# Order of the products' parts and of their reads in a fused graph-convolution and attention kernel on one core

## The chip, the core and the metric

The kernel runs on one core of a Trainium2 chip. The metric is the device time of one launch in microseconds. The kernel before took 2282.02 us (median of three runs, 2273.76 to 2284.43).

A core has a matrix engine (TensorE, PE in the profile; its weight loads are PEld), a vector engine (VectorE, DVE), an activation engine (ScalarE, ACT), a general engine (GpSimd, POOL) and a queue engine (SyncE, SP), from which this kernel issues all of its transfers. Each engine runs its own list of instructions in order, and they wait for each other by semaphores.

## The reference

Two layers on x of 128 graphs x 128 nodes x 512 features in fp32, each added to its own input:

```python
h = relu(layernorm(x))
norm_adj = adj * deg_inv_sqrt[:, None] * deg_inv_sqrt[None, :]
x = x + norm_adj @ (h @ weight) + bias

h = relu(layernorm(x))
q, k, v = (h @ W + b for W, b in ((Wq, bq), (Wk, bk), (Wv, bv)))     # 8 heads of 64
scores = q @ k.T / 8 + (1 - adj) * -1e9
x = x + softmax(scores) @ v @ Wo + bo
```

`adj` is one 128 x 128 matrix for all graphs. The five products with 512 x 512 weights are most of the work.

## The kernel before

Four graphs make a group; there are NG = 32 groups. The matrix products with weights multiply a 512 x 512 operand (four graphs, or their transpose) by a 512 x 512 weight.

Each such product is computed by Strassen-Winograd with seven half-size products P1, P5, P2, P6, P3, P7, P4 (`PRODUCTS`, line 31). Three of them (P1, P6, P7) are plain products of four 128 x 256 block matmuls, each in two halves of 64 output rows. The other four are themselves split: P5 and P3 by seven 128 x 128 block matmuls (`SEVEN`, line 80), P2 and P4 by another seven, cut into "phases" of four, two and one (`PHASES`, line 70). Sums of weights and of operands for this are made beforehand, mainly by GpSimd (`combine_one`, L91).

The results go to six PSUM banks: a0 and a1 by turns for the plain products, d0 and d1 for the seven (four blocks in d0, three in d1), b for P2 and c for P4. VectorE, and for first reads ScalarE, adds what the banks hold into the result in SBUF (`add` L437, `read` L447, `first` L726 and L740). Banks accumulate: P3 is added on top of P5 in d0 and d1, and a later phase on top of an earlier, and so a bank is read twice or three times, each time into the next place where Winograd's scheme needs the running sum. A matmul that goes on in a bank therefore has to wait until the reads of its state so far are over. In d0, four blocks lie side by side, and their reads are two columns of blocks (512 wide), single blocks (128 wide) and a diagonal of two blocks (256 wide).

`Projection.step(n)` issues product n's matmuls and its first reads, `rest(n)` the reads that come after whatever the plan has put between. Of P4, phases 1 and 2 are not issued in their own projection: they are kept in `tail` and issued at the start of steps 1 and 2 of the next projection, before that step's own matmuls; their reads follow in the same step. In the projection K the result of P4 is taken differently (`whole`: ScalarE reads part of bank c and adds the bias) and nothing trails.

The main loop goes over t = 0 to 32. In each t come five blocks of seven steps: W (graph convolution of group t + 1), Q, K and V (projections of group t) and Y (output projection of group t - 1). A written plan (`at(t, place, f)`) puts all other work at places such as "Q1" (before step 1 of Q), "Q1b" (between step 1 and its rest). The order of every engine is the order in which the program writes its instructions. The pieces that matter here:

- W3: on SP, the store of the second half of group t - 2 (`store_half` L853), whose last values are the trailing phases of Y read in W1 and W2. The load of the first half of x for group t + 2 (`load_x` L167) comes right after it on SP's queue, and that of the second half at W5.
- Q0b, Q1b, Q3b: the layer statistics of those loads (`ln1`: BATCH_NORM_STATS2 L322, aggregation L323, and L327), on VectorE. The trailing phases of W are issued and read in Q1 and Q2.
- K0b and K3b: statistics of group t + 1 after its convolution (`ln2`), for its first and second half. The normalised rows of the second half are made at V5 and V6.
- V0: attention times v of the group before (L835), then the scores of this group (L769), which VectorE masks and moves from PSUM (L776).
- Y6b or Y3b: the row maximum of the scores' last graph (`row_max` L788) on VectorE, just ahead of W.

Of the kernel before, what the change touches and what calls it, by code (L numbers as in the profile page):

```python
# [68 lines left out]

PHASES = (((0, 0, 0), (3, 6, 1), (2, 2, 2), (1, 1, 3)), ((6, 3, 3), (5, 5, 0)), ((4, 4, 0),))  # L70

# [23 lines left out]
def kernel(  # L95
# [288 lines left out]
    class Projection:  # L384
# [25 lines left out]

        def seven(self, product, fresh):
            i, k = product
            for x, y, b, place in SEVEN:
                self.matmul(
                    bank[f"d{b}"][:, place * P : (place + 1) * P],
                    self.left.slot(i, x),
                    self.right.slot(k, y),
                    fresh and place == 0,
                )

        def phase(self, out, product, n):
            i, k = product
            for m, (x, y, place) in enumerate(PHASES[n]):
                self.matmul(
                    out[:, place * P : (place + 1) * P],
                    self.left.slot(i, x),
                    self.right.slot(k, y),
                    n == 0 and m == 0,
                )
# [9 lines left out]
        @staticmethod  # L439
        def diagonal(dst):  # L440
            d0, d1 = dst[:, 0, 0, :], dst[:, 1, 1, :]
            return bass.AP(d0.tensor, d0.offset, [d0.ap[0], [d1.offset - d0.offset, 2], d0.ap[-1]])

        def read(self, half, y, src):
# [9 lines left out]

        def read_seven(self, half, y, part, first=False):
            dst = self.cut(half, y)
            diagonal = self.diagonal(dst)
            m = [bank[f"d{b}"].rearrange("p (s f) -> p s f", f=P) for b in range(2)]
            columns = m[0][:, 0:2].unsqueeze(2).to_broadcast([P, 2, 2, P])
            if part == 1:  # L460
                self.add(dst[:, 1, 0], m[0][:, 3])
                self.add(diagonal, m[1][:, 1:3])
                self.add(dst[:, 0, 1], m[0][:, 2])
                self.add(diagonal, m[0][:, 2:4], ALU.subtract)
                return
            if first and self.first is not None:
                self.first(dst.rearrange("p j r f -> p r j f"), columns, y)
            else:
                self.add(dst.rearrange("p j r f -> p r j f"), columns)
            self.add(diagonal, m[1][:, 0:1].to_broadcast([P, 2, P]))  # L470

        def read_phase(self, half, y, src, n):
            dst, m = self.cut(half, y), src.rearrange("p (s f) -> p s f", f=P)
            if n == 0:
                self.add(dst[:, :, 0], m[:, 0:2])
                self.add(self.diagonal(dst), m[:, 2:4])
            elif n == 1:
                self.add(dst[:, 0, 1], m[:, 3])
                self.add(dst[:, 0, 1], m[:, 0])
            else:  # L480
                self.add(dst[:, 1], m[:, 0:1].to_broadcast([P, 2, P]))

        def step(self, n):
# [3 lines left out]
            left = tail.pop(0) if n in (1, 2) and tail else None  # L487
            if left:

                left[0]()  # L490
            if n == 0:
# [3 lines left out]
            elif n == 1:  # L495
                if inner:
                    self.seven(P5, True)
                else:
                    self.product(bank["d0"], P5, True)
            elif n == 2:  # L500
                if inner:
                    self.phase(bank["b"], P2, 0)
                else:
                    self.product(bank["b"], P2, True)
            elif n == 3:
                self.product(a, P6, False)
                self.read_first(0, 1, a)
            elif n == 4:
                if inner:
                    self.phase(bank["b"], P2, 1)  # L510
                    if self.whole:
                        self.phase(m, P4, 0)
                    self.seven(P3, False)
                    self.read_phase(0, 0, bank["b"], 1)
                    if self.whole:

                        self.whole(t[:, 0, :], m[:, : 2 * P], 0)
                        self.whole(t[:, 1, P:], m[:, 3 * P :], 1)
                        self.add(t[:, 0, :P], m[:, 2 * P : 3 * P])
                else:  # L520
                    self.product(bank["d0"], P3, False)
            elif n == 5 and self.whole:
                self.phase(m, P4, 1)
                self.product(a, P7, False)
                self.whole(t[:, 1, :P], m[:, 3 * P :], 1)
                self.add(t[:, 1, :P], m[:, :P])
                self.add(t[:, 0, :], a[:, : 2 * P])
# [29 lines left out]
            else:  # L557
                self.product(bank["c"], P4, True)
                self.read(1, 0, bank["c"])
            if left:  # L560
                left[1]()
            if n == 2:
                if inner:
                    self.read_phase(0, 0, bank["b"], 0)
                else:
                    self.read(0, 0, bank["b"])

        def rest(self, n):

            inner = self.inner  # L570
            if n == 1:
                if inner:
                    self.read_seven(1, 1, 0, True)
                else:
                    self.read_first(1, 1, bank["d0"])
            elif n == 2 and inner:
                self.read_seven(1, 1, 1)
            elif n == 4:
                if inner:
                    self.read_seven(0, 1, 0)  # L580
                    self.read_seven(0, 1, 1)
                else:
# [280 lines left out]
    for t in range(-1, NG + 1):  # L863
# [47 lines left out]
        elif 1 <= t + 1 < NG and t >= 0:  # L911
            g = t + 1
            at(t, "K0b" if g < NG - 1 else "Q0b", ln2, g, 0)
            at(t, "K3b" if g < NG - 1 else "Q3b", ln2, g, 1)
            if g == NG - 1:
# [277 lines left out]
```

## Time and profile before

| what | us |
|---|---|
| median of three runs | 2282.02 |
| the profiled execution, whole | 2282.34 |
| its span, first to last instruction | 2280.6 |
| TensorE busy | 2249.9 |
| VectorE busy | 1865.0 |
| GpSimd busy | 1864.7 |
| ScalarE busy | 1391.1 |
| one 128 x 512 read of PSUM by VectorE | 0.68 |
| one 128 x 256 read | 0.42 |
| one 128 x 128 read | 0.28 |

Busy time is summed over the span. A matmul's end is modelled in this profile, so two matmuls that overlap in the pipeline leave no gap between them even where the second began late; the starts of the records are more exact. The granted TensorE clock was 0.998. The transfers moved 565.17 MB, and the 16 DMA engines were busy 83.3% of the time with the kernel's own queue.

### The profile page before, as it was taken

How to read it: one execution, taken by the hardware profiler on the slowest of the kernel's cores; microseconds unless marked ns; L12 is line 12 of the kernel's file. 1: busy time of each engine (PE TensorE's matmuls, PEld its weight loads, DVE VectorE, ACT ScalarE, POOL GpSimd, SP SyncE). 2: the span in 40 equal slices, each digit the busy share in tenths (PEclk: the TensorE clock that was granted, in tenths of full speed). 3: DMA queues.
4: the chain of work that ended last, by engine and by line, in shares of the span. 5: the costliest groups of instructions: out<-in, count | busy, mean ns of one | idle time of the engine just before them, and what ended most of it. 6: DMA issues, size and time to landing. Idle time of an engine off the chain costs nothing.

```text
span 2280.6 us, 79643 instructions
## 1 busy us (share of the span) xinstructions
PE 2249.9 (99%) x32679; PEld 1944.6 (85%) x32679; DVE 1865.0 (82%) x4832; ACT 1391.1 (61%) x3556; POOL 1864.7 (82%) x1928
## 2 busy tenths in 40 slices
PE   9899999999999999999999999999999999999999
PEld 7688888888888888888888888888888888888887
DVE  7778878888888788888888888888888888888876
ACT  4565666656656556666566665565755666655754
POOL 6899888878898788888888887889888888888764
PEclk9999999999999999999999999999999999999999
DMA  5388978889898898889898888988899988899882
GB/s 171 151 259 246 282 243 252 243 251 295 240 267 239 237 290 246 263 243 258 251 275 266 249 244 253 289 252 249 245 254 263 274 265 257 243 255 283 245 239 83
DMA packets 448700, 565.17 MB, mean 248 GB/s; under 512 B 326352, under 2 KB 333648, under 8 KB 447824
## 3 DMA queue, kind: packets, MB, share of 16 engines
q1 hardware_dynamic: 448336, 560.08, 83.3%
q8 instruction: 257, 4.21, 0.7%
q14 instruction: 107, 0.88, 0.1%
HBM read 358.68 MB, written 122.68 MB: 211 GB/s over the span
## 4 chain that ended last, share of the span: by engine, by line
PE 80%; DVE 8%; DMA 8%; issue 1%; POOL 1%; SPq 1%; ACT 0%; DVEq 0%; POOLq 0%
PE bank_a L137 29%; PE bank_d L137 17%; PE bank_b L137 9%; PE bank_c L137 8%; DMA xt<-in_x_dram 7%; PE pa L137 5%; DVE xt L437 3%; PE bank_d L769 3%; PE po L835 2%; DVE xt L447 2%; PE pt L686 1%; PE pss L769 1%; PE bank_b L835 1%; PE bank_a L835 1%; DVE nmx L788 1%
## 5 line engine op out<-in xcount | busy, mean ns | idle before, releaser
L796 ACT ACTIVATE att<-att,nmx 128x128 f32<-128x128 f32 x1024 | 396.5, 391 | 0.8 <-DVE nmx L788 0.8
L137 PE MATMUL bank_a<-op_h,w 128*64 128x256 f32 x2976 | 356.6, 380 | 0.0
L804 POOL TENSOR_TENSOR att<-att,rsm 128x1024 f32<-128x1024 f32 x128 | 242.9, 1898 | 61.0 <-DVE rsm L803 59.3
L137 PEld LDWEIGHTS bank_a<-op_h,w 128*64 128x64 f32 x2976 | 225.7, 137 | 67.0 <-issue 1.2
L437 DVE TENSOR_TENSOR xt<-xt,bank_d 128x512 f32<-128x512 f32 x732 | 268.9, 415 | 14.1 <-PE bank_d L137 0.5
L809 ACT COPY att<-att 128x2048 uint16<-128x2048 uint16 x121 | 229.3, 1895 | 54.4 <-POOL att L804 54.4
L341 ACT ACTIVATE h<-xt,nb,rs 128x512 f32<-128x512 f32 x254 | 207.4, 818 | 74.6 <-POOL nb L330 72.9
L328 POOL TENSOR_TENSOR rs<-ve,mhalf 128x2 f32<-128x2 f32 (+1 forms) x129 | 91.7, 711 | 181.9 <-DVE ve L327 181.2
L726 ACT ACTIVATE q<-bank_a,bqk 128x256 f32<-128x256 f32 x192 | 80.4, 470 | 247.2 <-PE bank_a L137 244.5
L91 POOL TENSOR_TENSOR op_o<-op_o 128x256 f32<-128x256 f32 x297 | 210.4, 733 | 10.0
L137 PE MATMUL bank_d<-op_h,w 128*64 128x128 f32 (+1 forms) x3424 | 215.4, 276 | 2.6 <-issue 0.4
L91 POOL TENSOR_TENSOR op_a<-op_a 128x256 f32<-128x256 f32 x279 | 197.1, 730 | 14.9 <-DVE op_a L373 5.2
L137 PEld LDWEIGHTS bank_d<-op_h,w 128*64 128x64 f32 x3424 | 193.6, 137 | 10.8 <-issue 7.1
L91 POOL TENSOR_TENSOR op_h<-op_h 128x256 f32<-128x256 f32 x270 | 191.0, 731 | 12.4 <-DVE op_h L373 3.1
L322 DVE BATCH_NORM_STATS2 st<-xt 128x6 f32<-128x512 f32 x256 | 173.2, 677 | 31.1 <-DMA xt<-in_x_dram 31.0
L796 ACT ACTIVATION_READ_ACCUMULATOR att<-att,nmx 128x1 f32 x1024 | 194.6, 190 | 0.0
L137 PE MATMUL bank_a<-w,op_o 128*64 128x256 f32 x1536 | 183.9, 379 | 0.0
L137 PE MATMUL bank_a<-w,op_h 128*64 128x256 f32 x1488 | 178.8, 381 | 0.0
L137 PE MATMUL bank_a<-w,op_a 128*64 128x256 f32 x1488 | 176.4, 379 | 0.0
L447 DVE TENSOR_TENSOR xt<-bank_a,xt 128x512 f32<-128x512 f32 x252 | 167.1, 684 | 9.6 <-PE bank_a L137 3.0
L776 DVE SCALAR_TENSOR_TENSOR att<-bank_d,msk 128x512 f32<-128x512 f32 x128 | 82.5, 686 | 102.2 <-PE bank_d L769 94.9
L788 DVE TENSOR_REDUCE nmx<-att 128x8 f32<-128x1024 f32 x128 | 154.9, 1210 | 0.0
(183 smaller groups left out, 5810.1 us busy)
## 6 DMA issues: line engine op xcount, KB each, us to landing
w<-wd_v SPq DMA_DIRECT2D x93, 704.0 KB, 5.9
w<-wd_o SPq DMA_DIRECT2D x93, 704.0 KB, 7.5
w<-wd_q SPq DMA_DIRECT2D x90, 704.0 KB, 6.5
planes<-att SPq DMA_DIRECT2D x121, 512.0 KB, 4.8
w<-wd SPq DMA_DIRECT2D x87, 704.0 KB, 5.8
xt<-in_x_dram SPq DMA_DIRECT2D x63, 512.0 KB, 6.2
out_dram<-xt SPq DMA_DIRECT2D x62, 512.0 KB, 4.4
planes_h<-att SPq DMA_DIRECT2D x29, 512.0 KB, 3.0
```

The source lines that it names most:

```text
L91: engine.tensor_tensor(twice(out), twice(x), twice(y), ALU.subtract if minus else ALU.add)
L137: nc.tensor.matmul(out[y : y + P // 2], lhsT[:, y : y + P // 2], rhs, **flags)
L322: nc.vector.bn_stats(self.st[:, j, :], self.src[:, j, :])
L328: nc.gpsimd.tensor_tensor(self.rs[:, c], self.ve[:, c], mhalf[:, c], ALU.pow)
L341: nc.scalar.activation(h, src[:, j, :], AF.Relu, bias=nb[:, j : j + 1], scale=rs[:, j : j + 1])
L437: nc.vector.tensor_tensor(dst, dst, src, f)
L447: nc.vector.tensor_tensor(t, src.rearrange("p (r f) -> p r f", r=2), t, ALU.add)
L788: nc.vector.tensor_reduce(nmx, att_of(g, b), AX.X, ALU.max, negate=True)
L796: nc.scalar.activation(att[:, h, :], att[:, h, :], AF.Exp, bias=nmx[:, h : h + 1], scale=1.0, accum_out=sm[:, h : h + 1])
L804: nc.gpsimd.tensor_tensor(att, att, rsm.unsqueeze(2).to_broadcast([P, H, P]), ALU.mult)
L809: nc.scalar.copy(planes, halves)
L835: nc.tensor.matmul(po[p * HD : (p + 1) * HD, c * P : (c + 1) * P], vs[g][:, b, h * HD : (h + 1) * HD], aT[:, p * NC + c, :], start=True, s ...
```

## The change

There are four parts.

- In `SEVEN`'s use: the blocks of one product are issued bank by bank. P5 (step 1) issues d0's four, then d1's three; P3 (step 4) d1's three first, then d0's four. Reads of d0 and d1 are split into `read_columns`, `read_three` (d1), `read_across` and `read_minus` and put in an order that begins with d1 (except for the columns in step 1). d1's first read moves from the rest of step 1 to the rest of step 2.
- The trailing phases: phase 1 is issued between d0's and d1's blocks in step 1, phase 2 behind P2's phase 0 in step 2, and the read of phase 2 behind that of bank b.
- `PHASES` gets new places in the bank, with an order of its own for projections whose weights stay (Q and K), so that the reads of the phases are four 256-wide instructions instead of five (three 256-wide and two 128-wide). Where weights don't stay, the two 128-wide reads of d0 become one of 256, too. In step 4 the second of phase 1's two reads goes behind the first read of d1.
- The second statistics of `ln2` go from K3b to K6b, except for the last group.

```diff
-PHASES = (((0, 0, 0), (3, 6, 1), (2, 2, 2), (1, 1, 3)), ((6, 3, 3), (5, 5, 0)), ((4, 4, 0),))
+PHASES = {
+    False: (((2, 2, 0), (0, 0, 1), (1, 1, 2), (3, 6, 3)), ((6, 3, 2), (5, 5, 1)), ((4, 4, 1),)),
+    True: (((2, 2, 0), (0, 0, 1), (3, 6, 2), (1, 1, 3)), ((6, 3, 3), (5, 5, 1)), ((4, 4, 1),)),
+}
...
-        def seven(self, product, fresh):
+        def seven(self, product, fresh, banks):
             i, k = product
-            for x, y, b, place in SEVEN:
+            for x, y, b, place in (s for c in banks for s in SEVEN if s[2] == c):
...
+        def across(self, dst):
+            return self.two(*((dst[:, 1, 0, :], dst[:, 0, 1, :])[:: 1 if self.stay else -1]))
...
+        def read_columns(self, half, y, first=False):
+            dst, _, _, columns = self.seven_parts(half, y)
             if first and self.first is not None:
                 self.first(dst.rearrange("p j r f -> p r j f"), columns, y)
             else:
                 self.add(dst.rearrange("p j r f -> p r j f"), columns)
-            self.add(diagonal, m[1][:, 0:1].to_broadcast([P, 2, P]))
...
+        def read_three(self, half, y, n):
+            _, diagonal, m, _ = self.seven_parts(half, y)
+            if n == 0:
+                self.add(diagonal, m[1][:, 0:1].to_broadcast([P, 2, P]))
+            else:
+                self.add(diagonal, m[1][:, 1:3])
+
+        def read_across(self, half, y, column):
+            dst, _, m, _ = self.seven_parts(half, y)
+            if not self.stay:
+                if column == 0:
+                    self.add(self.across(dst), m[0][:, 2:4])
+            elif column == 0:
+                self.add(dst[:, 1, 0], m[0][:, 3])
+            else:
+                self.add(dst[:, 0, 1], m[0][:, 2])
+
+        def read_minus(self, half, y):
+            _, diagonal, m, _ = self.seven_parts(half, y)
+            self.add(diagonal, m[0][:, 2:4], ALU.subtract)
+
+        def read_phase(self, half, y, src, n, part=(0, 1)):
             dst, m = self.cut(half, y), src.rearrange("p (s f) -> p s f", f=P)
             if n == 0:
-                self.add(dst[:, :, 0], m[:, 0:2])
-                self.add(self.diagonal(dst), m[:, 2:4])
+                self.add(self.diagonal(dst), m[:, 1:4:2] if self.stay else m[:, 1:3])
             elif n == 1:
-                self.add(dst[:, 0, 1], m[:, 3])
-                self.add(dst[:, 0, 1], m[:, 0])
+                if 0 in part:
+                    self.add(self.across(dst), m[:, 2:4])
+                if 1 in part:
+                    self.add(dst[:, 0], m[:, 0:2])
             else:
-                self.add(dst[:, 1], m[:, 0:1].to_broadcast([P, 2, P]))
+                self.add(dst[:, 1], m[:, 1:2].to_broadcast([P, 2, P]))
...
-            if left:
-
-                left[0]()
...
             elif n == 1:
                 if inner:
-                    self.seven(P5, True)
+                    self.seven(P5, True, (0,))
                 else:
                     self.product(bank["d0"], P5, True)
+                if left:
+                    left[0]()
+                if inner:
+                    self.seven(P5, True, (1,))
             elif n == 2:
                 if inner:
                     self.phase(bank["b"], P2, 0)
                 else:
                     self.product(bank["b"], P2, True)
+                if left:
+                    left[0]()
...
-                    self.seven(P3, False)
-                    self.read_phase(0, 0, bank["b"], 1)
+                    self.seven(P3, False, (1, 0))
+                    self.read_phase(0, 0, bank["b"], 1, (0,))
...
             elif n == 2 and inner:
-                self.read_seven(1, 1, 1)
+                self.read_three(1, 1, 0)
+                self.read_across(1, 1, 0)
+                self.read_three(1, 1, 1)
+                self.read_across(1, 1, 1)
+                self.read_minus(1, 1)
             elif n == 4:
                 if inner:
-                    self.read_seven(0, 1, 0)
-                    self.read_seven(0, 1, 1)
+                    self.read_three(0, 1, 0)
+                    self.read_phase(0, 0, bank["b"], 1, (1,))
+                    self.read_three(0, 1, 1)
+                    self.read_columns(0, 1)
+                    self.read_across(0, 1, 0)
+                    self.read_minus(0, 1)
+                    self.read_across(0, 1, 1)
...
-            at(t, "K3b" if g < NG - 1 else "Q3b", ln2, g, 1)
+            at(t, "K6b" if g < NG - 1 else "Q3b", ln2, g, 1)
```

## The prediction

> **What bounds the kernel now.** I read, in this order: the page's busy row, the waits by engine, the chain of waits in one iteration, and the timeline of that iteration. t is an iteration of about 69.9 us; W, Q, K, V, Y are its five blocks, a digit the product in it (0 to 6).
>
> ```profile
> PE 2249.9 (99%) x32679; PEld 1944.6 (85%) x32679; DVE 1865.0 (82%) x4832; ACT 1391.1 (61%) x3556; POOL 1864.7 (82%) x1928
> ```
>
> TensorE is the bound, and only holes in its stream can be won. The 99% hides them, because a matmul counts as busy until its modelled end. So I took the starts of all PE matmul records: a 128x128 block (four records) starts every 0.217 us and a 128x256 block every 0.433 us, and what exceeds these pitches is a hole. The holes come to 61 us. By the groups before and after, those the change touches are: bank_d to bank_c<-w,op_a (Q2) 13.2 us in 23 iterations; bank_b to bank_d in Q4 7.1 us (29); bank_d to bank_c in K5 4.5 us (28); bank_d to bank_c<-w,op_o (W2) 4.05 us (29); bank_b to bank_d in V4 2.6, W4 1.3, Y4 0.6 us; and three single ones, in the first Q1 (3.4), in the last K1 (0.75) and V1 (0.44).
>
> The waits by engine (total, times, longest) say who holds the largest, and what holds the holder:
>
> ```profile
> DVE att L776 <- PE bank_d L769: 94.9, 33, 4.5
> ...
> DVE st L322 <- DMA xt<-in_x_dram: 31.0, 29, 2.9
> ...
> PEld bank_c L137 <- DVE xt L437: 25.9, 54, 3.7
> ```
>
> VectorE waits for the load of x once an iteration, about 1 us, and the bank_c read that TensorE needs stands behind it. The chain of waits around 1231 to 1242 us closes the loop:
>
> ```profile
> 1230.60 1.14 DVE xt L437 x3
> ...
> 1231.86 8.60 DMA xt<-in_x_dram
> ...
> 1240.48 0.70 DVE st L322
> ...
> 1241.39 0.18 DVE xt L437
> ...
> 1241.60 0.30 DVE xt L437
> ...
> 1241.94 0.44 PE bank_c L137 x4
> ```
>
> The last bank_c read of W2 releases a store, the x load stands behind that store on SP's queue, it lands 8.6 us later, and only then do the statistics and the two bank_c reads of Q1 run. In the timeline of the same iteration, PE and DVE in Q1 to Q4, then K3 to K5:
>
> ```profile
> 1239.86 1.70 PE L137 MATMUL bank_d<-op_h,w 128*64 128x128 f32 x28
> ...
> 1241.94 0.44 PE L137 MATMUL bank_c<-w,op_a 128*64 128x128 f32 x4 [0.38 <-DVE xt L437]
> ...
> 1244.28 1.14 DVE L437 TENSOR_TENSOR q<-q,bank_d 128x128 f32<-128x128 f32 x4
> ...
> 1244.81 0.61 PE L137 MATMUL bank_b<-op_h,w 128*64 128x128 f32 x8
> ...
> 1245.52 1.75 PE L137 MATMUL bank_d<-op_h,w 128*64 128x128 f32 x28
> ...
> 1260.25 0.68 DVE L322 BATCH_NORM_STATS2 st<-xt 128x6 f32<-128x512 f32 x1
> ...
> 1262.58 0.28 DVE L437 TENSOR_TENSOR k<-k,bank_c 128x128 f32<-128x128 f32 x1
> ...
> 1262.91 0.66 PE L137 MATMUL bank_c<-op_h,w 128*64 128x128 f32 x8
> ```
>
> Each hole ends just after a DVE read: Q4's bank_d at 1245.52 after the last of four reads (1245.42), K5's bank_c at 1262.91 after the read that began at 1262.58.
>
> [...] Q4's first matmul writes bank_d0's first quarter, which nobody has read since Q1, and still waits for the last bank_d read of step 2. So seven blocks that start with bank d1 wait for d1's readers alone.
>
> **The change part by part.** DVE pitches below are starts of neighbouring DVE rows near 1231 and 1244 us: 256 wide 0.33 us, 0.45 if it depends on the one before; 128 wide 0.20; 512 wide 0.60; statistics and aggregation 0.72.
>
> Fewer reads. The build has 461 fewer DVE instructions: two 128-wide reads become one of 256, so 461 x (2 x 0.28 - 0.416) = 66 us of DVE busy time go. DVE isn't the bound, so this alone is worth nothing; it counts only where a hole waits behind it. PE has the same 16,928 matmuls, SP the same transfers in the same order, ACT the same instructions; POOL's order changes only once (t=1). PE gets 337 more semaphore waits. K4's bank_d already has a double wait and no hole, so I price them at 0 [...].
>
> W2 and Q2 (trailing phases later). Between the first and second trailing phase PE runs 1.52 us before and after: seven blocks before; three of d1 and four of bank_b after. What is won is that both come 0.87 us later against a landing that is fixed in time. Against it: the Q1 reads become two dependent 256s instead of two 128s, 0.87 for 0.57 us to their end, +0.29; and the store. In W1/W2, DVE is busy without a break from the row maximum at 1227.57. Before, c1, the columns and one diagonal stand ahead of the last bank_c read, which starts at 1230.94. After, the diagonal goes; the c1 pair ends 0.26 later, and bank_b's read must wait for its phase, done on PE at about 1230.58 plus the 0.25 that reads show after a group. So that read starts at 1230.85, the last bank_c read at 1231.18: store and load are +0.25 us. W2's own hole goes (c1 read ends 1230.17, PE arrives 1230.58). Where Q2 was held (20 iterations by over 0.2 us) the gain of W2 and Q2 together is 0.87 - 0.29 - 0.25 = 0.33 us, so 6.6; in the other 9 it is W2's hole, 0.14, so 1.3. Sum 7.9 us. Bounds: if the landing stays put, since it's set by the queue of bytes ahead of it, +0.25 x 20 = 13; if it lands 0.3 later still, 2.
>
> The single holes: the first is shortened by the four d0 blocks now ahead of the wait, 0.87; the other two go. 2.0 us.
>
> Q4. From the start of the Q1 bank_c reads to the end of the second d1 read DVE now needs 0.78 + 1.02 (second statistics) + 3 x 0.33 + 0.20 + 0.42 + 0.06 = 3.47 us; PE from there 0.93 to its phase, then 0.22 + 1.73 + 0.43 = 3.31. So 0.16 is left of 0.27 where Q2 is held: 20 x 0.11; in the others the hole goes, 9 x 0.2. d0 follows 0.65 later, and its last read ends 4.0 us from the start against 4.12 on PE: no new hole. 4.0 us; bounds 0 and 7.
>
> K5. The statistics that delay it (1260.25 to 1262.15) go to K6b. There DVE has been idle before the scores, 94.9 us in 33 waits, 2.9 us an iteration: 1.9 us fit, and POOL's part (1269.96) still starts after its own backlog. The bank_c read is then tied to ACT (1262.2), PE comes at 1262.75. 4.4 us; without that cover 1.9 us would delay each iteration's masks, not TensorE.
>
> V4, W4, Y4: d1 first and shorter reads; 4.0 of 4.5 us.
>
> Sum: 7.9 + 2.0 + 4.0 + 4.4 + 4.0 = 22.3 us. The profiled execution took 2282.34 us (span 2280.6), next to the median of 2282.02: forecast 2260.
>
> **Rivals.** (1) The landing stays put: 5 us more, 2255. For it: loads took 7.4 to 10.35 us for 512 KB, far over their own bytes, so a backlog sets them; against: the backlog is partly issued with PE. (2) The load lands 0.3 us later still: 6 less, 2266. (3) An engine that feeds PE takes over behind V: POOL, 82% busy, combines op_o until 1283.2, and V's inputs and Y follow. The gains of K5 and V4 would be lost, 2267. Against: Y1 needs it only at 1286.3. (4) The order of d0 and d1 doesn't count, since one counter for all DVE reads releases both: Q4 and V4 stay, 2267. (5) Slower: the later store puts the x load among the attention transposes and weight reloads. One mechanism, at Q1's statistics: each further microsecond of landing costs 29 us less 2.7 us of slack, and the gains are eaten at about 0.87 us. At 1.2 us: 2260 + 34.8 - 2.7 = 2292. For it: one load did take 10.35 us, 2 us over the usual 8.3; against: bytes and order are the same.
>
> **How the numbers follow.** Forecast 0.46, (1) 0.17, (2) 0.12, (3) 0.09, (4) 0.07, (5) 0.09. The range 2249 to 2275 holds the cases (1) to (4) with their bounds and leaves (5) and the far tail out. 0.5% is about what a measurement of this kernel can tell from no change: 11.4 us, so faster means below 2270.6. Some of (2) to (4) and a little of the forecast fall within it: faster 0.78, same 0.13, slower 0.09.
>
> **What would show it.** The wait of bank_c on DVE xt falls from 25.9 us to below 15; DVE still waits for x, 1 us or a little more an iteration, and the load follows its store by 0.48 us; K5's hole is gone and DVE's idle time before the scores falls from 94.9 to about 40 us; DVE busy falls by some 66 us and PE's matmul count stays. Q4's bank_d has a hole of 0.1 to 0.2 us in held iterations. I'm wrong if loads take over 9 us as a rule, if bank_d waits in Q4 as before, or if new waits of PE on POOL or ACT appear in V and Y.

## The result and the profile after

| | before | after |
|---|---|---|
| median, us | 2283.25 (7 runs, 2273.76 to 2286.8) | 2263.95 (7 runs, 2260.37 to 2266.97) |
| ratio, with its 95% interval | 1 | 0.992 (0.9901 to 0.9938) |
| the profiled execution, us | 2282.34 | 2266.76 |
| its span, us | 2280.6 | 2265.0 |

The kernel became 0.8% faster, 19 us by the medians and 15.6 us between the two profiled executions. The profiled execution of after is the second slowest of its seven. First the busy row of the page of after, then its waits by engine (total, times, longest):

```profile
PE 2231.4 (99%) x32679; PEld 1903.6 (84%) x32679; DVE 1799.0 (79%) x4371; ACT 1385.6 (61%) x3556; POOL 1867.5 (82%) x1928
```

```profile
DVE st L325 <- DMA xt<-in_x_dram: 58.6, 30, 3.1
...
DVE att L815 <- PE bank_d L808: 51.0, 32, 3.1
...
PEld bank_c L140 <- DVE xt L440: 13.7, 19, 1.5
...
PEld bank_c L140 <- DVE k L440: 9.5, 30, 0.3
...
PE po L874 <- DMA att<-planes: 7.1, 9, 1.6
```

VectorE has 461 instructions fewer and is busy for 66 us less. The wait of bank_c for VectorE's reads of xt fell from 25.9 to 13.7 us, and VectorE's idle time ahead of the scores from 94.9 to 51.0. Three rows grew. VectorE waits for x for 58.6 us, before 31.0; TensorE's bank_c waits for reads of k 30 times, about 0.3 us each, 9.5 us in all (before 6.7 us in 29); and the attention product po waits for its transposed blocks, 7.1 us in 9 waits (before 1.3 in one).

The chain of waits of one iteration shows that Q2 is held as before:

```profile
1216.97 1.09 DVE xt L440 x3
...
1218.23 8.53 DMA xt<-in_x_dram
...
1226.79 0.71 DVE st L325
...
1227.70 0.32 DVE xt L440
...
1228.04 0.43 DVE xt L440
...
1228.52 0.44 PE bank_c L140 x4
```

The last bank_c read of W2 releases the store, the load follows, takes 8.5 us, and behind it come one statistics instruction, two bank_c reads and the phase in Q2.

To see where the time went, I gave each run of matmul records on one bank its fixed pitch (54.3 ns for a 128x128 record, 108.25 ns for a 128x256 one, a quarter of the prediction's pitches; the median distance of starts four records apart is 218 and 432 ns in both traces) and summed what lies beyond it up to the next run, by stage. This counts more than the 61 us of single holes in the prediction: it takes in gaps below 0.03 us, the slower pair of records behind a hole (0.154 us in place of 0.103 in K6), and a few missing records. Its total fell from 91.1 to 75.5 us, by 15.6, just as the span did, so the table covers the whole difference.

| excess by stage, us | before | after | won |
|---|---|---|---|
| W2 | 5.8 | 0.2 | 5.6 |
| Q2 | 15.6 | 13.7 | 1.9 |
| Q4 | 8.1 | 5.4 | 2.7 |
| K5 | 7.0 | 0.3 | 6.7 |
| K6 | 0.3 | 8.7 | -8.4 |
| V4, W4, Y4 | 3.6, 3.1, 3.7 | 0.3, 0.3, 0.3 | 9.5 |
| second attention product (po, b = 3) | 2.9 | 9.8 | -6.9 |
| largest hole near the start of the run | 3.1 | 2.2 | 0.9 |
| all other | 37.9 | 34.3 | 3.6 |

The largest hole near the start stands in the first Q1 before, and ahead of the last step of a W after. Two stages lost: K6 and po. K6 in the timeline of after, TensorE and then VectorE:

```profile
1246.77 1.70 PE L140 MATMUL bank_d<-op_h,w 128*64 128x128 f32 x28
1248.30 0.61 PE L140 MATMUL bank_c<-op_h,w 128*64 128x128 f32 x8
...
1250.47 0.39 PE L140 MATMUL bank_b<-op_h,w 128*64 128x128 f32 x4
1250.93 0.44 PE L140 MATMUL bank_c<-op_h,w 128*64 128x128 f32 x4
```

```profile
1247.76 0.29 DVE L440 TENSOR_TENSOR k<-k,bank_c 128x128 f32<-128x128 f32 x1 [1.22 <-ACT k L768]
...
1248.62 2.06 DVE L440 TENSOR_TENSOR k<-k,bank_d 128x256 f32<-128x256 f32 x5
1250.60 0.28 DVE L440 TENSOR_TENSOR k<-k,bank_c 128x128 f32<-128x128 f32 x1
```

K5's bank_c phase is computed by 1248.91, but its read starts at 1250.60, behind five reads of bank_d. TensorE would be ready for bank_c again at 1250.69 and starts at 1250.93, just after that read.

### The profile page after: what moved, and what is told of

It reads as the page before. It is cut to its first block, busy times and chain, and to the rows that moved or that the text cites. A ratio compares the mean times of both kernels' runs of the same rounds, so it can differ in the third digit from the quotient of the medians.

```text
span 2265.0 us, 79243 instructions
## 1 busy us (share of the span) xinstructions
PE 2231.4 (99%) x32679; PEld 1903.6 (84%) x32679; DVE 1799.0 (79%) x4371; ACT 1385.6 (61%) x3556; POOL 1867.5 (82%) x1928
## 3 DMA queue, kind: packets, MB, share of 16 engines
q1 hardware_dynamic: 448336, 560.08, 84.7%
## 4 chain that ended last, share of the span: by engine, by line
PE 75%; DMA 13%; DVE 6%; SPq 2%; ACT 1%; issue 1%; POOL 1%; DVEq 0%; POOLq 0%
PE bank_a L140 27%; PE bank_d L140 16%; PE bank_b L140 9%; PE bank_c L140 8%; DMA xt<-in_x_dram 7%; PE pa L140 4%; DMA planes<-att 3%; DVE k L440 3%; PE bank_d L808 3%; PE po L874 2%; DMA att<-planes 2%; DVE xt L440 2%; SPq L852 2%; PE pt L725 1%; PE pss L808 1%; PE bank_b L874 1%
## 5 line engine op out<-in xcount | busy, mean ns | idle before, releaser
L140 PEld LDWEIGHTS bank_a<-op_h,w 128*64 128x64 f32 x2976 | 208.2, 137 | 81.9 <-issue 1.2
L140 PE MATMUL bank_d<-op_h,w 128*64 128x128 f32 (+1 forms) x3424 | 223.0, 275 | 0.9 <-DVE q L440 0.9
L325 DVE BATCH_NORM_STATS2 st<-xt 128x6 f32<-128x512 f32 x256 | 173.2, 676 | 58.6 <-DMA xt<-in_x_dram 58.6
L348 POOL TENSOR_TENSOR xt<-xt,b 128x1024 f32<-128x1024 f32 (+1 forms) x65 | 153.1, 2358 | 0.0
```

Of the source, the lines that this page charges most:

```text
L140: nc.tensor.matmul(out[y : y + P // 2], lhsT[:, y : y + P // 2], rhs, **flags)
L325: nc.vector.bn_stats(self.st[:, j, :], self.src[:, j, :])
L348: nc.gpsimd.tensor_tensor(t, t, bias.unsqueeze(1).to_broadcast([P, t.shape[1], D]), ALU.add)
```

## The experiments

Medians, ratios against the kernel before (with intervals), and the same excess by stage, from the profiled execution of each:

| kernel | median us | ratio | Q2 | Q4 | K5 | K6 | V4+W4+Y4 | po | total |
|---|---|---|---|---|---|---|---|---|---|
| before | 2283.25 | 1 | 15.6 | 8.1 | 7.0 | 0.3 | 10.4 | 2.9 | 91.1 |
| after | 2263.95 | 0.992 (0.9901 to 0.9938) | 13.7 | 5.4 | 0.3 | 8.7 | 0.9 | 9.8 | 75.5 |
| undo_stats | 2274.93 | 0.9976 (0.9962 to 0.9989) | 8.5 | 5.1 | 14.0 | 13.2 | 0.9 | 3.4 | 82.2 |
| undo_trailing | 2275.27 | 0.9978 (0.9968 to 0.9988) | 30.9 | 1.2 | 0.3 | 8.8 | 0.9 | 0.5 | 78.0 |
| undo_order | 2305.71 | 1.0117 (1.01 to 1.0134) | 18.0 | 20.5 | 0.3 | 23.8 | 16.1 | 0.7 | 116.8 |
| reads_apart | 2260.45 | 0.9912 (0.9888 to 0.9936) | 14.5 | 5.6 | 0.3 | 8.9 | 0.9 | 2.2 | 68.7 |
| k_fix | 2251.05 | 0.9869 (0.9852 to 0.9886) | 11.9 | 5.3 | 0.3 | 0.4 | 0.9 | 5.6 | 62.0 |
| stats_behind | 2262.42 | 0.9923 (0.9906 to 0.9939) | 0.2 | 18.8 | 0.3 | 8.8 | 0.9 | 1.3 | 68.9 |
| load_first | 2258.72 | 0.9905 (0.9881 to 0.9928) | 0.2 | 2.0 | 0.3 | 15.2 | 0.9 | 22.1 | 80.5 |
| load1_later | 2283.17 | 1.0006 (0.9993 to 1.0019) | 11.3 | 5.2 | 0.3 | 8.8 | 0.9 | 0.7 | 90.0 |
| wv_later | 2253.36 | 0.9885 (0.9868 to 0.9903) | 10.9 | 4.7 | 0.3 | 8.8 | 0.9 | 1.3 | 63.1 |
| two_fixes | 2246.48 | 0.9854 (0.9835 to 0.9873) | 11.5 | 5.8 | 0.3 | 0.1 | 0.9 | 1.8 | 57.8 |
| three_fixes | 2239.83 | 0.9832 (0.9812 to 0.9853) | 1.1 | 2.0 | 0.3 | 0.3 | 0.9 | 5.3 | 47.6 |

Every kernel has the same matmuls, and its own queue moves the same 560.08 MB. Two limits of this table matter below. First, the kernel before was run again beside each group of experiments, on another chip each time, with medians of 2279.65 to 2283.18 us. A difference from after by medians, as given below, can therefore be off by some 3 us; where it matters, the ratios are used. Second, the stages come from one execution each, and po varies where nothing in an edit bears on it. In reads_apart and stats_behind SP's queue is as in after, and yet po stands at 2.2 and 1.3 us and not at 9.8. The wait for the transposed blocks, 7.1 us in 9 times in after, is this in reads_apart, and then in stats_behind:

```profile
PE po L879 <- DMA att<-planes: 0.5, 1, 0.5
```

```profile
PE po L874 <- DMA att<-planes: 0.4, 1, 0.4
```

The last transposing transfer ahead of the second attention product lands 27.9 us after the start of Q0 on the mean in after, and 27.3 and 26.6 us in these two. So a part of po's 9.8 us may well belong to that one execution of after and not to its order of instructions.

### Undoing the four parts

**undo_stats.** The second half of the statistics back from K6b to K3b:

```diff
-            at(t, "K6b" if g < NG - 1 else "Q3b", ln2, g, 1)
+            at(t, "K3b" if g < NG - 1 else "Q3b", ln2, g, 1)
```

> The kernel after, with the second half of the attention block's statistics back at K3b (all other parts of the change kept). Theory A (the K5 hole alone was the cost, as in the prediction): K5's hole is back at about 5 us, K6's hole of 7.2 us stays, time 2268. Theory B (all of VectorE's reads of K4 to K6 stand in one row, so the statistics delay every one behind them): in the trace of after VectorE is idle for 1.60 and 1.22 us in K3 and K4, 1.9 us of statistics fill the gaps and leave about 0.45 us of delay to every later read of K, which both the K5 and the K6 hole take over, 0.45 x 28 = 12.6 us, time 2276. If the move of the statistics was worth nothing: 2264.

Measured: 2274.93 us, 11 more. K5 and K6 both grew, by 13.7 and 4.5 us, as theory B said, and the time agrees with its 2276. But the way there is another, so the agreement is in part luck. K6 grew by 0.16 us in each iteration and not by 0.45, and K5 is not held evenly. In 19 of 29 iterations the hole is 0.05 us or less, in ten 1.16. The timelines of one of these, VectorE, GpSimd and TensorE:

```profile
1114.32 1.28 DVE L330 TENSOR_SCALAR ve<-mv 128x2 f32<-128x2 f32 x1
1115.52 0.41 DVE L440 TENSOR_TENSOR k<-k,bank_b 128x256 f32<-128x256 f32 x1
1115.85 0.27 DVE L440 TENSOR_TENSOR k<-k,bank_c 128x128 f32<-128x128 f32 x1
```

```profile
1114.31 1.27 POOL L376 TENSOR_TENSOR op_a<-op_a 128x512 f32<-128x512 f32 x1
```

```profile
1116.17 0.66 PE L140 MATMUL bank_c<-op_h,w 128*64 128x128 f32 x8 [0.98 <-DVE k L440]
```

The last small instruction of the statistics, 128x2, takes 1.28 us in place of its usual 0.17. It began 0.01 us after a GpSimd operation and ends with it, and the read that TensorE needs stands behind it. So the statistics were worth moving, though more than half of their harm in this kernel (ten times 1.1 us) is not their own length but the 1.1 us that this small instruction took longer beside GpSimd. In the kernel before, which has them at the same place, no iteration has a K5 hole over 0.27 us.

**undo_trailing.** The trailing phases issued at the start of steps 1 and 2 again, their reads ahead of bank_b's:

```diff
             elif n == 1:
+                if left:
+                    left[0]()
                 if inner:
                     self.seven(P5, True, (0,))
-                if left:
-                    left[0]()
-                if inner:
                     self.seven(P5, True, (1,))
...
             elif n == 2:
+                if left:
+                    left[0]()
                 if inner:
                     self.phase(bank["b"], P2, 0)
...
-                if left:
-                    left[0]()
...
+            if left:
+                left[1]()
             if n == 2:
...
-            if left:
-                left[1]()
```

> The kernel after, with the two trailing phases back at the start of steps 1 and 2 and their reads ahead of bank_b's; all else as after. Theory A (the prediction's: against a landing of x that is fixed in time the later place wins 0.87 us in a held iteration, of which 0.25 was given back by the later store): Q2's hole grows from 12.6 to about 25 us, W2's hole is back at 4 to 9 us, the load is issued 0.25 us earlier against Q0, time 2280 to 2285. Theory B (x follows the place of the trailing phase one for one, so only W2's hole was won): Q2's hole stays at about 13, W2's is back, time 2268 to 2271.

Measured: 2275.27 us, 11 more, between the two expectations. Q2 rose by 17 us to 30.9, more than theory A said, and W2's hole did not come back (0.5 us). Part of it was repaid: Q4 fell by 4.2 us, with TensorE later, and po by 9.3, of which a part may be the scatter named above. (The profiled execution, 2269.48 us, is one of the lowest of 22, so the stages sum to less than the medians say.) In the timeline of TensorE:

```profile
1228.68 1.70 PE L140 MATMUL bank_d<-op_h,w 128*64 128x128 f32 x28
1231.59 0.44 PE L140 MATMUL bank_c<-w,op_a 128*64 128x128 f32 x4 [1.21 <-DVE xt L440]
```

TensorE could go on at 1230.2, and the phase waits until 1231.59. The load is issued 6.17 us ahead of Q0 on the mean of 28 iterations, in after 5.25, yet lands only 0.24 us earlier against Q0 (2.96 and 3.20 us after its start). In stats_behind and reads_apart, where load and store stand as in after, it lands after 2.99 and 3.28 us. So the landing hardly followed an issue that is 0.92 us earlier, and what it did follow by is no more than the scatter between executions.

**undo_order.** The seven blocks of step 4 with bank_d0 first again, in all four projections:

```diff
-                    self.seven(P3, False, (1, 0))
+                    self.seven(P3, False, (0, 1))
```

> The kernel after, with the seven blocks of step 4 in the old order (bank_d0 first) in all four projections. Theory A (the order counts, for each bank is waited for by itself): step 4's first block waits for the last read of bank_d0, 0.53 us behind that of bank_d1, Q4's hole grows from 3.9 to some 15 to 19 us, holes of 3 to 10 us in all are back in V4, W4 and Y4, and the hole ahead of bank_c in K6 (7.2 + 1.5 us), which comes from bank_d0 being computed last, goes: 2264 + 13 + 7 - 9 = 2275, at least 2268. Theory B (all VectorE reads release a wait together, the order of the banks does not count): Q4, V4, W4 and Y4 stay as in after, K6's hole goes all the same, 2255.

Measured: 2305.71 us, 42 more, and slower than the kernel before. Q4 rose to 20.5 and V4, W4 and Y4 to 16.1 us: the order counts, theory A, and its share was under-estimated. In 29 of 30 iterations Q4's bank_d starts 0.10 to 0.15 us behind the end of the last bank_d read of step 2, just as it does in the kernel before. One part of the expectation was wrong. K6 did not close; it rose to 23.8 us. TensorE and VectorE in K:

```profile
1270.73 1.73 PE L140 MATMUL bank_d<-op_h,w 128*64 128x128 f32 x28
...
1275.40 0.44 PE L140 MATMUL bank_c<-op_h,w 128*64 128x128 f32 x4 [0.57 <-DVE k L440]
```

```profile
1272.49 0.42 DVE L440 TENSOR_TENSOR k<-k,bank_d 128x256 f32<-128x256 f32 x1 [0.48 <-PE bank_d L140]
```

The reads of step 4 begin with bank_d1. With bank_d1 computed last, even the first of them waits for the end of all seven blocks, and the whole row of reads, with bank_c's at its end, moves back. The order of the products and the order of the reads have to be changed together, as the change does. It also means that the 42 us are more than the order of the products is worth by itself: here it stands against reads that fit the other order.

**reads_apart.** Each read of two crossing blocks in two halves, which gives VectorE the 4832 instructions of the kernel before:

```diff
-                    self.add(self.across(dst), m[0][:, 2:4])
+                    self.add_apart(dst, m[0], 2)
...
-                    self.add(self.across(dst), m[:, 2:4])
+                    self.add_apart(dst, m, 2)
...
+        def add_apart(self, dst, m, place):
+            blocks = (dst[:, 1, 0], dst[:, 0, 1])[:: 1 if self.stay else -1]
+            for n, block in enumerate(blocks):
+                self.add(block, m[:, place + n])
```

> The kernel after, with each 256-wide read of two crossing blocks taken apart into two 128-wide ones, so that VectorE has as many instructions as in the kernel before (461 more, about 66 us more busy time); place and order of everything else as in after. Theory A (a read counts only where TensorE waits behind it): each pair costs 0.07 to 0.12 us more at the places that hold TensorE, so W2's hole comes back with up to 0.1 us in 29 iterations, Q2, Q4 and K6 grow by 0.1 us each where they are held, V4, W4 and Y4 stay closed: 2 to 8 us in all, time 2266 to 2272. Theory B (VectorE's load as such is what slows TensorE): a large part of the 66 us, 2285 or more. If the reads are worth nothing at all: 2264.

Measured: 2260.45 us (2254.0 to 2272.11), which cannot be told from after: neither theory's amount, and none of B. Q2, Q4 and K6 rose by 0.8, 0.2 and 0.2 us; W2 stayed shut. VectorE's busy time is 1819.5 us, 20.5 more than after, and not 66. The smaller number of reads is worth nothing here that can be measured, to within the 5 us or so of the interval. po fell to 2.2 us, for which the edit gives no reason.

reads_apart has as many reads of every width as the kernel before, and VectorE is still busy for 45.5 us less. So this part of the 66 us comes from the order of the reads, in which neighbours overlap more: a read right behind a 256-wide one starts 0.34 us after it on the mean, in the kernel before 0.36; behind a 128-wide one it is 0.20 and 0.23 us.

### The hole in K6

**k_fix.** K's bank_c read of step 5 ahead of the last three bank_d0 reads of step 4:

```diff
                     self.read_columns(0, 1)
-                    self.read_across(0, 1, 0)
-                    self.read_minus(0, 1)
-                    self.read_across(0, 1, 1)
+                    if not self.whole:
+                        self.rest_of_d0()
...
                 self.add(t[:, 1, :P], m[:, P : 2 * P])
+                self.rest_of_d0()
```

> The kernel after, where in K the read of bank_c of step 5 is put on VectorE right behind the read of bank_d0's columns, ahead of the three other reads of bank_d0 (same instructions, other order). Theory A (the new hole ahead of bank_c in K6 comes from VectorE's order: that read stands behind the d0 reads, which start late because d0 is now computed last): the read starts at about 0.85 us earlier, the hole of 0.245 us in each iteration is gone, 7.2 + 1.5 = 8.7 us, time 2255. Theory B (the hole is ScalarE's or TensorE's own, for instance the reading of bank_c by ScalarE): hole and time stay, 2264. If the three postponed reads of bank_d0 then hold the scores of V0: the hole moves there, 2262 or more.

Measured: 2251.05 us, 13 less than after. K6 is shut, 0.4 us of 8.7: theory A. VectorE, then TensorE:

```profile
1248.11 0.28 DVE L440 TENSOR_TENSOR k<-k,bank_c 128x128 f32<-128x128 f32 x1
1248.31 0.81 DVE L440 TENSOR_TENSOR k<-k,bank_d 128x128 f32<-128x128 f32 x3
```

```profile
1248.83 0.39 PE L140 MATMUL bank_b<-op_h,w 128*64 128x128 f32 x4
1249.05 0.39 PE L140 MATMUL bank_c<-op_h,w 128*64 128x128 f32 x4
```

The bank_c read ends 0.66 us before the phase that overwrites it, which now follows bank_b's after 0.22 us, its plain pitch. The three postponed reads held nothing. po and Q2 fell too, by 4.2 and 1.8 us, which makes up the difference to the expected 8.7; that the edit caused these two is not shown. By the ratios k_fix is 12 us below after, and the intervals do not meet.

### The wait for x in Q2

**stats_behind.** The first statistics of x behind the two bank_c reads of Q1 and not ahead of them:

```diff
-                at(t, "Q0b", ln1, g, 0, (0,), ())
+                at(t, "Q1b", ln1, g, 0, (0,), ())
```

> The kernel after, with the first statistics of x moved on VectorE from ahead of the two bank_c reads of Q1 to behind them (Q0b to Q1b); no transfer is moved. Theory A (Q2's hole is nothing but VectorE's order: the reads stand behind an instruction that waits for x): Q2's hole of 12.6 us goes to below 2 although x lands as before, Q4's of 3.9 to about 1; TensorE then comes to the attention product earlier and the waits for the transposed blocks grow from 9.6 us to as much as 20, time 2250 to 2260. Theory B (x itself is late for what follows, its scale and the normalised blocks): a hole of the same size comes up later in Q, 2264.

Measured: 2262.42 us, no difference that can be told. Q2's hole is gone (0.2 us) with x landing as before, and Q4 has risen to 18.8: theory A for Q2, and B in its outcome. Theory A's other half failed: Q4 did not fall, and po, which was to grow, fell to 1.3. VectorE and TensorE:

```profile
1225.99 0.88 DVE L440 TENSOR_TENSOR xt<-xt,bank_c 128x256 f32<-128x256 f32 x2 [2.02 <-PE bank_c L140]
1226.79 0.69 DVE L325 BATCH_NORM_STATS2 st<-xt 128x6 f32<-128x512 f32 x1
...
1229.27 1.47 DVE L440 TENSOR_TENSOR q<-q,bank_d 128x256 f32<-128x256 f32 x5
```

```profile
1230.26 1.75 PE L140 MATMUL bank_d<-op_h,w 128*64 128x128 f32 x28 [0.41 <-DVE q L440]
```

The two bank_c reads now run as soon as TensorE has written the bank, but the two statistics then stand ahead of Q2's reads of bank_d, and Q4 starts at 1230.26, just behind the second read of bank_d1, the third of the five. VectorE's wait for x fell from 58.6 to 3.5 us in this kernel, and the time didn't move: what holds TensorE is the work of VectorE between the start of Q1 and Q4, not that wait alone.

**load_first.** The first half's load ahead of the store in SP's queue:

```diff
-            at(t, "W3" if t > 1 else "W0", load_x, t + 2, (0,))
+            at(t, "W2" if t > 1 else "W0", load_x, t + 2, (0,))
```

> The kernel after, with the first half's load of x ahead of the store in SP's queue (at W2 instead of W3). Theory A (the landing of x follows its issue): the load is issued 0.5 to 0.85 us earlier against Q0 (from -5.25 to about -6 us), lands at +2.6 instead of +3.3 us after Q0's start, the hole ahead of bank_c in Q2 falls from 12.6 us to 2 to 4 us, time 2255. Theory B (the landing is set by the bytes queued ahead): it lands where it did, time 2264. In both, if the waits of the attention product for the transposed blocks (7.1 us in 9 waits) follow SP's queue and not x, they stay, since the second half's load still waits there for the store.

Measured: 2258.72 us; its six runs spread from 2252 to 2272, and by its interval it can't be told from after. In the trace theory A holds: the load is issued 6.5 us ahead of Q0 and lands 1.7 us after its start (3.2 in after), Q2 and Q4 fall to 0.2 and 2.0 us. But po and K6 rise to 22.1 and 15.2 (the latter takes in a wait ahead of the first attention product). The profiled execution is the slowest of the six (clock 0.995, the others 0.998 to 1.000), so it shows the loss rather large. Its waits:

```profile
DVE st L325 <- DMA xt<-in_x_dram: 18.7, 26, 2.8
...
PE po L874 <- DMA att<-planes: 15.6, 14, 2.7
```

### The waits for the transposed blocks

The chain of waits at the end of K in one iteration of after, and SP's queue in the same iteration:

```profile
1309.70 8.42 DMA planes<-att
...
1318.14 4.83 DMA att<-planes
...
1323.11 0.95 PE po L874 x13
```

```profile
1287.49 0.65 SPq L170 DMA_DIRECT2D xt<-in_x_dram  x1
...
1294.81 0.37 SPq L170 DMA_DIRECT2D xt<-in_x_dram  x1
1295.24 1.05 SPq L1058 DMA_DIRECT2D w<-wd_v  x1
1296.34 5.65 SPq L852 DMA_TRANSPOSE att<-planes  x1
1302.09 0.53 SPq L1058 DMA_DIRECT2D w<-wd_v  x1
1302.66 5.84 SPq L852 DMA_TRANSPOSE att<-planes  x1
1308.59 0.53 SPq L849 DMA_DIRECT2D planes<-att  x1
...
1312.24 7.83 SPq L852 DMA_TRANSPOSE att<-planes  x2
```

The second half's load waits in the queue until the store before it has landed (5.9 us, until 1294.8; 150.4 us in 28 such waits in the whole run). Then the first two transposing transfers occupy the queue for 5.65 and 5.84 us, the planes of blocks 2 and 3 come after the second one, and the last transpose lands at 1323.0. ScalarE had ended its last two copies before these planes at 1303.27 and 1307.37; the queue reached them at 1308.59 and 1309.70.

**load1_later.** The second half's load behind the first transposing transfer:

```diff
-            at(t, "W5" if t > 1 else "W0", load_x, t + 2, (1,))
+            at(t, "Q1" if t > 1 else "W0", load_x, t + 2, (1,))
```

> The kernel after, with the second half's load of x moved in SP's queue from W5 (where it blocks the queue for about 6 us until the store has landed) to behind the first transposing transfer (Q1). Theory A (the new waits of the attention product for its transposed blocks, 7.1 us in 9 waits, come from SP's queue being later): the transposes are issued 3 to 5 us earlier, these waits go, 2255 to 2257. Theory B (they come from x through ScalarE's later copies): the waits stay, 2264. Theory C (the transpose then shares the time with the first half's load and x lands later): the hole ahead of bank_c in Q2 grows by more than is won, 2270 or more.

Measured: 2283.17 us, 19 more. po's excess is gone (0.7 us), as theory A said; since it is small in stats_behind and reads_apart too, and TensorE comes later here, this alone does not show that SP's queue is its cause. And the whole gain of the change is lost elsewhere, as theory C had it, but at another place than it said. The waits:

```profile
DVE st L325 <- DMA xt<-in_x_dram: 126.1, 58, 3.6
...
PE bank_b L140 <- DVE q L440: 21.3, 20, 1.8
```

Now the second half of x lands late. VectorE waits for it in 28 more places, with step 4's reads of bank_b in Q behind it, and TensorE loses 24.9 us at the phase in Q6; Q2 didn't grow.

**wv_later.** The same aim without touching x: two of the reloads of the value weights behind the transposing transfers:

```diff
-            "W": ((t, "W6"), (t, "Q4"), (t, "Q1"), (t, "K3")),
+            "W": ((t, "Q2"), (t, "Q4"), (t, "Q6"), (t, "K3")),
```

> The kernel after, with two of the four reloads of the value weights moved in SP's queue from ahead of the transposing transfers 0 and 1 to behind them and behind the writing of the last planes (W6 to Q2, Q1 to Q6). Theory A (the second attention product waits because the transposes stand behind other transfers and their bytes in SP's queue): transposes 0 and 1 land 2 to 4 us earlier, the last one 1 us or more, the excess ahead of the second product falls from 9.6 to 3 us or less, time 2257. Theory B (it's set by when ScalarE copies the planes): it stays, 2264. Theory C (the weights then come too late for V): new waits of TensorE on the weights' transfer, above 2264.

Measured: 2253.36 us, 10.6 less than after. po's excess is 1.3 us of 9.8, as theory A said, and no wait of TensorE for weights came up. Against Q0 the last transpose is issued 1.0 us earlier on the mean and lands 0.9 us earlier. But in stats_behind, with SP's queue untouched, it is issued 1.2 and lands 1.3 us earlier. So theory A is in line with the trace and not shown by it. The gain in time is better founded: the slowest run here is below the fastest of after. By the ratios it is 8 us, with intervals that just meet.

### Together

**two_fixes** and **three_fixes** combine k_fix and wv_later, the second with load_first too.

> The kernel after with both fixes that no other stage paid for: K's bank_c read ahead of the last three bank_d0 reads, and two value-weight reloads behind the transposes. If their gains add: 2264 - 13 - 10.5 = 2240.5. If part of each is the same wait for the transposed blocks (its excess fell from 9.6 to 5.5 us with the first fix alone, and to 1.2 with the second): 2264 - 8.7 - 8.4 - 2.7 (Q2's hole, as it fell with the reloads) = 2244. In both K6 and the second attention product have no hole, and Q2's hole of about 10 us stays.

> The same two fixes, and the first half's load of x ahead of the store. Theory A (with the transposes issued early the attention product no longer takes back what Q2 wins): Q2's hole of about 10 us and Q4's of 3 to 4 us go, and the second attention product has less than 4 us of excess, time 2230 to 2233. Theory B (TensorE comes earlier and meets the transposes again, as with the earlier load alone, where that excess grew from 9.6 to 20 us): time 2238 to 2244, no better than without the earlier load.

Measured: 2246.48 and 2239.83 us. By the medians the two fixes do not add in full: 17.5 us less than after, where the sum is 23.5 (15 and 20 by the ratios, which the intervals do not tell apart). A part of k_fix's gain may have been the same wait for the transposed blocks; its po stood at 5.6 us. The third brings 6.7 us by the medians, with intervals that overlap a little, so between the theories. Waits of three_fixes:

```profile
DVE st L325 <- DMA xt<-in_x_dram: 21.1, 28, 2.6
...
PE po L879 <- DMA att<-planes: 2.4, 3, 1.5
```

Against two_fixes, Q2 won 10.4 us and Q4 3.8, and po took 3.5 back. three_fixes is the best version that was run: 0.9832 of the kernel before, and 24 us below after.

## Why the prediction came out right, step by step

The forecast was 2260 us, the time 2263.95 (the profiled execution 2266.76), and the direction and the range held. But the sum was nearly right by luck, because its errors cancel: 22.3 us were foreseen, and in the two profiles 31 us were won and 15 lost, which leaves 15.6.

- **W2 and Q2**, foreseen 7.9 us: 7.5. The size is right, the reasons only in part. W2's 5.6 us do not hang on the later trailing phase: with the old place its hole stayed shut (undo_trailing), and with the reads apart too. Either edit is enough for it, or a third one is; neither was tried without the other. In Q2 the later place is worth 17 us, of which Q4 and po gave 13.5 back in the profiles. The store and load were foreseen 0.25 us later; against Q0 the issue moved by 0.59 and the landing by 0.60 us (from 2.60 to 3.20 us after its start). VectorE's wait for x was to stay at 1 us or a little more an iteration; it became 2 us.
- **Single holes**, foreseen 2.0: less than half came. The first was not shortened but moved: from 95 to 125 us of the run the excess is 6.1 us before and 5.6 after, with holes of 2.4 us in W and 1.6 us at Q1 in place of the 3.4 us at Q1. The one in K1 is gone; near that in V1 (0.47 us) one of 0.67 us stands now.
- **Q4**, foreseen 4.0: 2.7. In 22 of 30 iterations 0.12 us of hole is left, against the 0.16 foreseen. But 25 iterations are held by 0.05 us or more and not 20, two of them by 0.65 us.
- **K5**, foreseen 4.4: the hole is gone and 6.7 us with it. This is right as far as it goes, and undo_stats shows the move was needed, if mostly for a small instruction that took 1.28 us and not 0.17 beside GpSimd, which the prediction did not know of.
- **K6**, not in the sum: it lost 8.4 us. Here the prediction failed. It followed K5's bank_c read up to the phase in K5 and stopped there; with bank_d0 computed last, its four reads moved behind K5's start, and the next bank_c read stands behind them. k_fix shows that their order alone is the cause.
- **V4, W4 and Y4**, foreseen 4.0: 9.5. The mechanism was right, and undo_order shows it: 15 us return there, more than the change won, since the reads then fit the other order. The term was mis-sized, since the holes were counted only where they passed 0.03 us: of the 10.4 us before, 6.0 stand ahead of step 4's blocks, where 4.5 were counted, and 4.4 within them, as the pair of records behind each hole is 0.05 us slow as well.
- **The attention product**, not in the sum: 6.9 us lost in that profile. The order on SP was said to be the same, which it is, but against Q0 everything behind the later store on SP came later. This would be rival (5)'s kind of mechanism at another place, the transposes and not the statistics of x, and smaller. How much of the 6.9 us it is stays open, since po is 1.3 and 2.2 us in two kernels with the same order on SP.
- **Fewer reads**: no worth of their own, as foreseen. The 66 us were worked out from 0.28 and 0.416 us for the two widths, the medians in the trace of before. The figure agreed with the trace by chance: the 461 instructions account for 20.5 us, and the other 45.5 come from the order of the reads, as reads_apart shows.
- **TensorE's further waits**, priced at 0. The trace of after has 93 more wait instructions on TensorE's queue (668, before 575), and one lasts 0.05 us there: near 5 us if none of it is hidden, an estimate from these two numbers. No stage shows a loss by them.

Rival (1), a landing that stays put, did not come true for the change, since it moved by 0.60 us; in undo_trailing it nearly did stay put, so how the landing follows the issue is open. That a backlog sets it is not shown; in the trace of before the second halves, 512 KB too, landed 3.5 to 5.9 us after their issue. Rival (2), a landing 0.3 us later than foreseen, came true with 0.35. Its 2266 us is the time of the profiled execution, but by chance, since K6 and po are not in it. Rival (3) did not come about: the gains of K5, V4, W4 and Y4 stayed. Rival (4), that the banks' order does not count, is refuted by undo_order: with bank_d0 first, Q4's bank_d starts 0.10 to 0.15 us behind the end of the last bank_d read in 29 of 30 iterations, and Q4 stands at 20.5 us in place of 5.4. In this program TensorE waits for the readers of the bank it writes.

## What to carry to other kernels

When an engine's reads run in a fixed order, a product that is moved to the end takes its reads with it: follow the row of reads past the hole that was closed, up to the next write of every bank that is read behind them (here K6, 8.4 us lost). A hole closed on the bound engine makes it arrive earlier at what follows (in load_first, Q2 fell from 13.7 to 0.2 us and po rose from 9.8 to 22.1), so look for the next transfer that only just arrived in time, and ask what stands ahead of it in its queue. Before a wait on a transfer is put down to an edit, look at the same wait in kernels that leave the transfer alone (po: 9.8 us in after, 1.3 and 2.2 in two kernels with the same queue). Moving a waiting instruction behind others wins nothing when the same work then stands ahead of the next reads (stats_behind: Q2 fell to 0.2 us, Q4 rose to 18.8).

## What the runs showed that was not expected

- The 128x2 instruction that ends the statistics takes 0.17 us, and in ten iterations of undo_stats 1.28 us, where it starts just behind the start of a GpSimd 128x512 operation. In all ten it ended 0.02 to 0.03 us behind GpSimd's, and the reads of PSUM around it kept their 0.41 us. In the kernel before, eleven of these small instructions began while GpSimd was at work. They took 0.25 to 1.45 us, and all eleven ended 0.02 to 0.03 us behind it; the others took 0.15 to 0.17. One such case cost an iteration 1.1 us on TensorE. Why the small instruction ends with GpSimd's, these traces do not show.
- The first transposing transfer of an iteration keeps SP's queue for 5.5 us in after (median of 30, up to 9.1), and for 8.7 us in load1_later, where it stands right behind the first load and two weight reloads; the fourth keeps it for 2.2 us in after (median). Others wait in line although their data is ready: the planes above were copied at 1303.27 and 1307.37, and the queue reached them 5.3 and 2.3 us later.
- In K6 and in step 4 a hole of TensorE costs about 0.05 us more than its length. In K6 of after the second pair of records behind the hole comes after 0.154 us; in the kernel before, where there is no hole, after 0.103. In Q4, V4, W4 and Y4 of before, the fourth record of bank_d behind a hole starts 0.167 us after the first; in V4, W4 and Y4 of after, without a hole, 0.116.
